# A graph network layer on one core: the node slices move from SyncE's queue to ScalarE's, SyncE copies more rows, and the end of the run is reordered

## The chip, the cores and the metric

One core of a Trainium2 chip. The metric is the time of one execution in device microseconds. Engines are named as in the profile: PE (TensorE), DVE (VectorE), ACT (ScalarE), POOL (GpSimd), SP (SyncE).

## The reference

One message-passing layer with a residual and a normalisation, on 12500 nodes of 64 features and 400000 edges with 16 attributes, sorted by `dst`:

```
m_in     = concatenate([x[src], x[dst], edge_attr], -1)
h        = silu(m_in @ W1 + b1)
messages = silu(h @ W2 + b2)
agg      = segment_sum(messages, dst, num_segments=12500)
y        = silu(concatenate([x, agg], -1) @ W3 + b3)
out      = layernorm(x + y)
```

## The kernel before

**Tiles and octets.** 128 edges are a tile, eight tiles an octet (1024 edges); there are 391 octets, the last of five tiles. Three octets make a chunk. Since `dst` is sorted, an octet's edges end in a window of 48 consecutive nodes. The table `pa = x @ W1[:64]` is made once, in DRAM.

**Four ways to the rows of `pa` for an octet's 1024 sources.** Most tiles are fetched by POOL, one indirect DMA a tile (`gather`, L448). Some pairs of tiles come another way, spread evenly: ACT and DVE put columns of x together in SBUF, one instruction a column (`columns`, L350 reads addresses into registers, L367 and L369 do the work), and SP copies single rows of `pa`, one DMA a row (`rows`, L393 reads 32 addresses, L397 copies). `ROWS` sets how many rows SP copies an octet: 256/15 = 17.07. A pair of tiles that comes one of these ways saves POOL two gathers.

**An octet's way through the engines.** SP loads the slice of x for the octet's window of nodes (`window_load`, L463 to L467; into one of three buffers xr) and, once a chunk, the edge attributes into the lower part of the tile oh (`load`, L485; two buffers, so that a chunk's load follows the last use of the chunk before the previous one). PE multiplies the slice (`window_product`, L472); DVE compares destinations and PE transposes the result (`turn`, L515), DVE copies it into oh (L525). The first layer (`first_layer`) is transposes of the fetched rows (L550), column products (L553) and one large product (L554); ACT makes h of it (L557). The second layer (L566, L568) goes to ACT for m (L572), into a single PSUM buffer p2. PE adds m up by node (`add_up`, L581), DVE adds the window into agg (`add_window`, L592). Finished groups of nodes pass through the last layer and the normalisation and are stored by SP (`store`, L664).

**The order of work.** A loop written by hand (from L757) sets the order on PE, ACT, DVE and SP; POOL's gathers go out ahead. Iteration o issues, among others: the slice for octet o+3, the oh load for the chunk that begins with octet o+3 (when one does, so in every third iteration), gathers for octet o+3, `turn` and `window_product` for o+1, the first layer of o with h, the second layer of o-2 with m, the adding up of o-4, and row copies. On ACT an iteration is: 24 columns, h, 16 columns, m. The oh load of iteration o waits for PE's first layer of octet o-1.

**Eight semaphores.** Every transfer that SP or ACT issues raises one of eight semaphores, named DMAHW0 to DMAHW7 in the listing of the built program. They are given out in turn to the transfers of both engines, in one order that the scheduler makes of the whole program. A transfer waits on its engine until the transfer before it on the same semaphore has landed. Where a row of the listing reads `[waits DMAHW2_49]`, this is that wait.

**The end.** The last iterations use shorter distances (`DRAIN`). `QUIET` keeps the last octets free of columns. At o = 390 the group of nodes `rest` and a check of limits are done, and the window additions of the folding step 391 come in the next turn of the loop; then come the last group, the verdict, the stores, and a load of the verdict on every engine (L106) for the branch into a general version that these inputs don't need.

```
def window_load(o):
    if o % 4 == 0:
        bases(ENG.SP, o)
    xr = xrs[o % 3]
    nc.sync.dma_start(xr[:D, :].bitcast(U8), xt2b[:, ds(winreg.pop((ENG.SP, o)), 8 * S)])
```

Of the kernel before, what the change touches and what calls it, by code (L numbers as in the profile page):

```python
# [12 lines left out]
U8 = mybir.dt.uint8  # L13
# [5 lines left out]
ENG = mybir.EngineType  # L19

P = 128
G = 4
CT = 24
OT = 8
S = 48
# [8 lines left out]
TABLES = 7  # L34
ACOLS = (48, 32)
VCOLS = (32, 0, 32, 32)
ROWS = (256, 15)
LOADS = (16, 32)
XADDR = 16640
X2ADDR = XADDR + 50528  # L40
AADDR = X2ADDR + 50016
HALF = 6144
OVER = 304
TURN = 195
QUIET = 5
DRAIN = 8
LAG = CT * P // 32
AHEADS = 256
# [6 lines left out]
@with_exitstack  # L55
def kernel(
    ctx: ExitStack,
    tc: tile.TileContext,
    x: bass.AP,
    xt: bass.AP,  # L60
    xt2: bass.AP,
    src_c: bass.AP,
    src_row: bass.AP,
    src_pair: bass.AP,
    dst_c: bass.AP,
    dst_row: bass.AP,
    attr_t: bass.AP,
    attr_2: bass.AP,
    base: bass.AP,
    w1: bass.AP,  # L70
    b1: bass.AP,
    w2: bass.AP,
    b2: bass.AP,
    w3: bass.AP,
    b3: bass.AP,
    out: bass.AP,
    edges: int,
):

    nc = tc.nc
    N, D = x.shape

    const = ctx.enter_context(tc.tile_pool(name="const", bufs=1))
    dram = ctx.enter_context(tc.tile_pool(name="dram", bufs=1, space=DRAM))
    pa = dram.tile([N, D], F32, name="pa")
    badi = const.tile([1, 1], I32, name="badi")
    ident = const.tile([P, P], F32, name="ident")
    make_identity(nc, ident)
    identb = const.tile([P, P], BF16, name="identb")  # L100
    nc.vector.tensor_copy(identb, ident)

    with ExitStack() as inner:
        windows(inner, tc, ident, identb, badi, pa, x, xt, xt2, src_c, src_row, src_pair, dst_c, dst_row, attr_t, attr_2, base, w1, b1, w2, b2, w3, b3, out, edges)

    flag = nc.values_load(badi[0:1, 0:1], min_val=0, max_val=4 * P,  # L106
                          skip_runtime_bounds_check_because="a count of partitions")
    with tc.If(flag > 0):
        general(tc, ident, x, xt, src_c, dst_c, dst_row, attr_t, w1, b1, w2, b2, w3, b3, out, edges)


def windows(ctx, tc, ident, identb, badi, pa, x, xt, xt2, src_c, src_row, src_pair, dst_c, dst_row, attr_t, attr_2, base, w1, b1, w2, b2, w3, b3, out, edges):
    nc = tc.nc
    N, D = x.shape
# [3 lines left out]
    NO = base.shape[1]  # L118
# [18 lines left out]
    bi = fast.tile([1, NO], I32, name="bi")  # L137
# [83 lines left out]
    NA = max(HALF + OVER, N - HALF + S)  # L221
# [27 lines left out]
    bi8 = bf.bitcast(I32)  # L249
# [45 lines left out]
    with tc.tile_pool(name="gat", bufs=AHEAD + 2) as gat, \  # L295
# [32 lines left out]
        for eng in counts:  # L328
            pairs[eng] = []
            for o in range(len(octs) - QUIET - 2):  # L330
                if counts[eng][o] >= 2 * P * (len(pairs[eng]) + 1):
# [43 lines left out]
        def rcount(o):  # L375
            return max(0, o - RAW) * ROWS[0] // ROWS[1]

# [57 lines left out]
        winrow, winreg = {}, {}  # L435
        xt2b = xt2.bitcast(U8)
# [16 lines left out]
        def bases(eng, o):  # L453

            n = min(4, NO - o)
            at, least, most = (bi8, 0, 8 * (N - 1)) if eng == ENG.SP else (bi, AADDR, AADDR + 4 * (NA - S))
            _, regs = nc.values_load_multi_w_load_instructions(
                at[0:1, o:o + n], engines=(eng,), min_val=least, max_val=most,
                skip_runtime_bounds_check_because="dst names a node")
            for i in range(n):  # L460
                winreg[eng, o + i] = regs[i]

        def window_load(o):  # L463
            if o % 4 == 0:
                bases(ENG.SP, o)
            xr = xrs[o % 3]
            nc.sync.dma_start(xr[:D, :].bitcast(U8), xt2b[:, ds(winreg.pop((ENG.SP, o)), 8 * S)])  # L467
            winrow[o] = xr

        def window_product(o):  # L470
# [89 lines left out]
        def second_layer(o):  # L560
            c, t0, n, first, last = octs[o]
            n2 = n + n % 2
            k = n2 // 2
            h, eh = made.pop(o)
            p2 = ps2.tile([P, OT, D], F32, name="p2")
            nc.tensor.matmul(p2[:, :n2, :], one3, b2r[:, :n2, :], start=True, stop=False, skip_group_check=True)  # L566
            for i in range(k):
                nc.tensor.matmul(p2[:, 2 * i:2 * i + 2, :].rearrange("p s d -> p (s d)"), h[:, i, :], w2d,  # L568
                                 start=False, stop=(i == k - 1), skip_group_check=True)
            columns(o + 1, ENG.Activation, 1)  # L570
            m = msg.tile([P, OT, D], F32, name="m")
            nc.scalar.activation(m[:, :n2], p2[:, :n2], AF.Silu)  # L572
            made[o] = m, eh

        def add_up(o):
            c, t0, n, first, last = octs[o]
            m, eh = made.pop(o)
            pg = sums[:, o % 4, :]
            for i in range(n):
                s = i % 2  # L580
                nc.tensor.matmul(pg[s * D:(s + 1) * D, :], m[:, i, :], eh[:, i // 2, :, s],  # L581
                                 start=(i < 2), stop=(i >= n - 2), skip_group_check=True)
# [4 lines left out]
        def add_window(o):  # L587
            if o == TURN:
                nc.vector.tensor_copy(agg[:, :OVER], agg[:, HALF:HALF + OVER])
                clear(HALF, NA)  # L590
            a = agg.bitcast(U8)[:, ds((winreg.pop((ENG.DVE, o)) - AADDR).with_bounds(min_val=0, max_val=4 * (NA - S), guaranteed_mod_val=0, out_of_modulus=4), 4 * S)].bitcast(F32)
            nc.vector.tensor_tensor(a, a, sums[:, o % 4, :], op=OP.add)  # L592
# [4 lines left out]
        NG = len(groups)  # L597
        RB = 5
        v = nv.tile([P, 2 * RB, G, D], F32, name="v")
# [56 lines left out]
        def divide(q, i):  # L656
            p = groups[q][1] // G
            vi = v[:p, q % (2 * RB), i, :]
            j = q * G + i
            nc.vector.tensor_scalar(vi, vi, mv[:p, j, 0:1], rstd[:p, j:j + 1], op0=OP.subtract, op1=OP.mult)  # L660

        def store(q):
            c, n = groups[q]
            nc.sync.dma_start(out[c:c + n, :].rearrange("(p i) d -> p i d", i=G), v[:n // G, q % (2 * RB)])  # L664

# [11 lines left out]
        for q in range(rest):  # L679
            o = lead[due[q]] + LAST - 1  # L680
# [10 lines left out]
        for q0, q1 in batches:  # L691
            o = lead[due[q1 - 1]] + LAST + 2 * G
# [27 lines left out]
        def verdict(bad):  # L720
            pc = mis.tile([1, 4], F32, name="mm")
            nc.tensor.matmul(pc, onec, bad, start=True, stop=True)
            bs = nv.tile([1, 1], F32, name="bs")
            nc.vector.tensor_reduce(bs, pc, AX.X, OP.add)
            nc.vector.tensor_copy(badi, bs)

        def times(lags):

            at = {}
            for o in range(NO):  # L730
                at.setdefault(o + lags.get(NO - 1 - o, lags[None]), []).append(o)
            return at
# [3 lines left out]
        folds = times({None: LAST, **{k: 3 for k in range(DRAIN)}})  # L736
# [17 lines left out]
        with tc.manual_schedule(engines={ENG.PE, ENG.Activation, ENG.DVE, ENG.SP}):  # L754
# [4 lines left out]
            for o in range(NO + 2):  # L759
# [3 lines left out]
                for k in range(0, NA, XC)[3 * o - 3:3 * o] if o else []:  # L763
                    n = min(XC, NA - k)
# [33 lines left out]
                for b in range(0, NO, 4):  # L798
                    if o == b + (4 if b < NO - DRAIN else 2):
                        bases(ENG.DVE, b)  # L800
                for q in folds.get(o, []):
                    add_window(q)
                if o == 1:
                    relative(0, CT, SCT)
                for k in range(3 * o - 3, 3 * o) if 1 <= o < 6 else []:
                    if k < 2 * len(parts):
                        c = parts[k // 2]
# [5 lines left out]
                def behind():  # L813
                    for q in adds.get(o, []):
                        add_up(q)
                    for q in seconds.get(o, []):
                        second_layer(q)

                if o == NO - 1:
                    assert NG == rest + 2 and groups[rest][0] + groups[rest][1] + LAG <= (NO - 4) // (CT // OT) * STEP  # L820
                    behind()
                    for i in range(G):
                        node_sums(rest, i)
                    node_silu(rest)
                    node_add(rest)
                    for i in range(G):
                        node_stats(rest, i)
                    bad = limits()
# [42 lines left out]
                if o in (NO - 4, NO - 3):  # L871
                    q = rest + (o == NO - 3)
# [4 lines left out]
            for i in range(NO + 2, NO + LAST):  # L877
                for q in folds.get(i, []):
                    add_window(q)
            assert NO not in todo  # L880
            for i in range(G):
                node_sums(rest + 1, i)
            node_silu(rest + 1)
            node_add(rest + 1)
            for i in range(G):
                node_stats(rest + 1, i)
            verdict(bad)
            root(rest, NG)
            inverse(rest, NG)
            for q in range(rest, NG):  # L890
                for i in range(G):
                    divide(q, i)
                store(q)


@with_exitstack
def general(ctx, tc, ident, x, xt, src_c, dst_c, dst_row, attr_t, w1, b1, w2, b2, w3, b3, out, edges):
# [9 lines left out]
    assert turns * U * P == edges  # L907
    ROWS = N + P

# [3 lines left out]
    pb = dram.tile([N, D], F32, name="gpb")  # L913
    accs = [dram.tile([ROWS, D], F32, name=f"acc{k}") for k in range(NACC)]

# [34 lines left out]
    with tc.tile_pool(name="gpre", bufs=3) as pre, tc.tile_pool(name="zero", bufs=1) as zp, \  # L950
            tc.tile_pool(name="gpre_ps", bufs=4, space=PSUM) as pps:
        width = ROWS * D // P
        assert width * P == ROWS * D
        zero = zp.tile([P, width], F32, name="zero")
# [197 lines left out]
```

## Time and profile before

| | |
|---|---|
| median of 3 runs | 3294.95 us (3292.81 to 3297.97) |
| profiled execution | 3292.35 us, span 3290.6 us |
| mean granted TensorE clock | 0.708 |
| gathers of POOL (L448), both tables | 2599 |
| row copies of SP (L397) | 6400 |
| slices (L467), oh loads (L485) | 391, 132 |
| columns of ACT (L367), of DVE (L369) | 14464, 16000 |

Busy times leave out DMA issues and register loads; these stand in the timeline as SPq and ACTq. A group's row gives its total busy time, the mean of one instruction, the idle time before it and what ended most of that. In the rows of a source line the three numbers are the shortest, the median and the longest duration in ns. A row of a window gives its length and then busy time of PE, PEld, DVE, ACT and POOL, the granted clock, and the DMA share.

### The profile page before, as it was taken

What the parts mean: (1) busy time and instruction counts of PE and PEld (TensorE: products, weight loads), DVE (VectorE), ACT (ScalarE), POOL (GpSimd) and SP (SyncE); (2) the same over time, 40 slices, a digit from 0 to 9 for tenths busy, and PEclk for the clock granted to TensorE, in tenths of its full rate; (3) what the DMA queues carried; (4) which work ended last, traced back from release to release, by engine and by line L of the source; (5) the groups of instructions that cost most, each with busy time, mean ns of one, the idle gap of its engine ahead of it and who ended that gap; (6) DMA issues with size and microseconds to landing.
All of it is one profiled execution on the core that took longest, in us unless ns stands there. A gap on an engine that the chain in (4) does not pass through costs nothing. (4 is left out here: it accounts for less than half of the span.)

```text
span 3290.6 us, 88339 instructions
## 1 busy us (share of the span) xinstructions
PE 2486.1 (76%) x15344; PEld 1705.0 (52%) x15344; DVE 2042.4 (62%) x18296; ACT 3109.2 (94%) x15306; POOL 2465.6 (75%) x2607
## 2 busy tenths in 40 slices
PE   7867777777777777767777777777877867777786
PEld 5545555555555545544454554545545545554554
DVE  5566666666666666666666666666666666666652
ACT  2799999999999999999999999999999999999991
POOL 7777777777777777777777777777777777777774
PEclk8787777777667677677767767766666676667666
DMA  7222222222222222221221222222222222222221
GB/s 148 50 41 40 43 41 40 43 41 40 45 44 44 42 42 40 41 43 38 48 46 39 43 41 40 43 43 43 45 41 42 40 44 41 43 44 45 39 42 33
DMA packets 160868, 147.82 MB, mean 45 GB/s; under 512 B 103748, under 2 KB 113718, under 8 KB 159526
## 3 DMA queue, kind: packets, MB, share of 16 engines
q0 software_dynamic: 83168, 85.33, 14.6%
q1 hardware_dynamic: 62624, 47.00, 5.7%
q10 hardware_dynamic: 14502, 9.75, 1.4%
q14 instruction: 447, 3.66, 0.4%
q8 instruction: 127, 2.08, 0.3%
HBM read 135.44 MB, written 6.40 MB: 43 GB/s over the span
## 5 line engine op out<-in xcount | busy, mean ns | idle before, releaser
L448 POOL DMA_INDIRECT ga<-pa,sc x2505 | 2375.6, 948 | 763.9 <-issue 666.0
L367 ACT ACTIVATE cx<-xs,x 128x1 f32 x14464 | 2789.5, 328 | 24.9 <-issue 19.5
L369 DVE TENSOR_TENSOR cx<-xs,x 128x4 uint8 x16000 | 1288.9, 154 | 1095.6 <-issue 1073.7
L581 PEld LDWEIGHTS pg<-eh,m 128*64 128x64 f32 x6250 | 296.8, 184 | 674.5 <-DVE agg L592 344.5
L550 PE MATMUL p<-ident,ga 128*128 128x128 f32 x1253 | 347.1, 364 | 393.7 <-DMA ga<-pa,sc 392.6
L568 PEld LDWEIGHTS p<-w2d,h 128*128 128x128 f32 x3126 | 536.7, 259 | 186.5 <-issue 186.5
L568 PE MATMUL p<-w2d,h 128*128 128x128 f32 x3126 | 632.5, 365 | 0.0
L554 PE MATMUL p<-oh,xw 128*128 128x512 f32 (+1 forms) x758 | 584.6, 866 | 0.0
L581 PE MATMUL pg<-eh,m 128*64 128x48 f32 x6250 | 352.8, 271 | 211.4 <-DVE agg L592 209.1
L550 PEld LDWEIGHTS p<-ident,ga 128*128 128x128 f32 x1253 | 220.4, 186 | 468.4 <-issue 433.2
L557 ACT ACTIVATE h<-p 128x512 f32<-128x512 f32 x391 | 243.1, 622 | 53.5 <-PE p L554 33.1
L515 PE MATMUL ph<-identb,eh 128*96 128x128 bf16 x1563 | 211.9, 276 | 99.9 <-DVE oh L525 96.4
L572 ACT ACTIVATE m<-p 128x512 f32<-128x512 f32 x391 | 242.6, 620 | 41.6 <-PE p L568 40.0
L525 DVE COPY oh<-ph 96x512 f32<-96x512 f32 x391 | 263.1, 673 | 1.9 <-PE ph L515 1.9
L515 PEld LDWEIGHTS <-eh 128*96 128x96 bf16 x1563 | 163.4, 163 | 136.5 <-DVE oh L525 122.4
L566 PE MATMUL p<-b2r,one 3*128 3x512 bf16 x391 | 193.3, 494 | 53.7 <-ACT m L572 53.2
L472 PE MATMUL mm<-w1bb,xr 65*96 65x128 f32 x782 | 221.5, 377 | 6.6 <-DMA xr<-in_xt 4.0
L497 DVE TENSOR_TENSOR eh<-wrow,dc 128x384 f32<-128x384 f32 x392 | 212.5, 542 | 11.3 <-PE wrow L624 6.9
L554 PEld LDWEIGHTS p<-oh,xw 128*128 128x128 f32 x758 | 175.8, 284 | 0.0
L472 PEld LDWEIGHTS mm<-w1bb,xr 65*96 65x96 f32 x782 | 139.9, 230 | 8.1 <-DMA xr<-in_xt 4.2
L553 PE MATMUL p<-cx,w1d 128*128 128x128 f32 x474 | 122.1, 368 | 0.0
L477 DVE TENSOR_TENSOR xw<-mm,mask 96x128 f32<-96x128 f32 x391 | 108.1, 276 | 20.6 <-PE mm L472 18.0
(106 smaller groups left out, 980.1 us busy)
## 6 DMA issues: line engine op xcount, KB each, us to landing
rx<-pa SPq DMA_DIRECT2D x6400, 0.2 KB
ga<-pa,sc POOLq DMA_INDIRECT x2505
oh<-in_attr SPq DMA_DIRECT2D x130, 192.0 KB
xr<-in_xt SPq DMA_DIRECT2D x391, 24.0 KB
cxi<-in_src_pair SPq DMA_DIRECT2D x238, 1.0 KB
xs<-in_xt ACTq DMA_DIRECT2D x6, 512.0 KB
pa<-v ACTq DMA_DIRECT2D x12, 256.0 KB
x<-in_xt ACTq DMA_DIRECT2D x6, 512.0 KB
```

Of the source, the lines that this page charges most:

```text
L367: nc.scalar.activation(cols[key][:, k:k + 1], word(i, xb, XADDR), AF.Identity, bias=word(i + 4, x2b, X2ADDR))
L369: nc.vector.tensor_tensor(t[:, 4 * k:4 * k + 4], at(i, xb, XADDR), at(i + 4, x2b, X2ADDR), op=OP.max)
L448: nc.gpsimd.indirect_dma_start(out=ga[:, i, :], out_offset=None, in_=x if o < RAW else pa[:, :], in_offset=bass.IndirectOffsetOnAxis(ap=sc ...
L472: nc.tensor.matmul(pw[:E, :], winrow[o], w1bb.rearrange("k s m -> k (s m)"), start=True, stop=True)
L515: nc.tensor.matmul(ph[:E, i, :], eh[:, i, :, 1], identb, start=(i == 0), stop=(i == k - 1), skip_group_check=True)
L525: nc.vector.tensor_copy(oh[:E, :], ph[:E, :(n + 1) // 2].rearrange("p i e -> p (i e)"))
L550: nc.tensor.matmul(p1[:, i, :], g2.rearrange("p s d -> p (s d)"), ident, is_transpose=True, start=(i == c), stop=False, skip_group_check=True)
L554: nc.tensor.matmul(p1[:, :k], xw[o % 3], oh, start=False, stop=True, skip_group_check=True)
L557: nc.scalar.activation(h[:, :k], p1[:, :k], AF.Silu)
L568: nc.tensor.matmul(p2[:, 2 * i:2 * i + 2, :].rearrange("p s d -> p (s d)"), h[:, i, :], w2d, start=False, stop=(i == k - 1), skip_group_ch ...
L572: nc.scalar.activation(m[:, :n2], p2[:, :n2], AF.Silu)
L581: nc.tensor.matmul(pg[s * D:(s + 1) * D, :], m[:, i, :], eh[:, i // 2, :, s], start=(i < 2), stop=(i >= n - 2), skip_group_check=True)
```

## The change

- `window_load` and the register loads of its addresses (`bases`) go to ACT's queue.
- `ROWS` goes from 256/15 to 256/14: 18.29 rows an octet; 26 pairs of tiles instead of 25 come by rows. `QUIET` goes from 5 to 3: one more pair comes by DVE's columns. POOL's gathers from `pa` go from 2505 to 2501.
- At the end: the window additions of step 391 move ahead of the group `rest`, the verdict ahead of the last group's sums, the load of the flag ahead of the last store, and the last store (53 partitions) is split into 48 and 5.

```diff
-ROWS = (256, 15)
+ROWS = (256, 14)
...
-QUIET = 5
+QUIET = 3
...
-            at, least, most = (bi8, 0, 8 * (N - 1)) if eng == ENG.SP else (bi, AADDR, AADDR + 4 * (NA - S))
+            at, least, most = (bi8, 0, 8 * (N - 1)) if eng != ENG.DVE else (bi, AADDR, AADDR + 4 * (NA - S))
...
             if o % 4 == 0:
-                bases(ENG.SP, o)
+                bases(ENG.Activation, o)
             xr = xrs[o % 3]
-            nc.sync.dma_start(xr[:D, :].bitcast(U8), xt2b[:, ds(winreg.pop((ENG.SP, o)), 8 * S)])
+            nc.scalar.dma_start(xr[:D, :].bitcast(U8), xt2b[:, ds(winreg.pop((ENG.Activation, o)), 8 * S)])
...
-            nc.sync.dma_start(out[c:c + n, :].rearrange("(p i) d -> p i d", i=G), v[:n // G, q % (2 * RB)])
+            to, p = out[c:c + n, :].rearrange("(p i) d -> p i d", i=G), n // G
+            for a, b in ((0, p // 16 * 16), (p // 16 * 16, p)):
+                if b > a:
+                    nc.sync.dma_start(to[a:b], v[a:b, q % (2 * RB)])
...
-                for q in folds.get(o, []):
+                for q in folds.get(o, []) if o != NO else []:
                     add_window(q)
...
                     behind()
+                    for q in folds[NO]:
+                        add_window(q)
                     for i in range(G):
                         node_sums(rest, i)
...
+            verdict(bad)
             for i in range(G):
                 node_sums(rest + 1, i)
...
-            verdict(bad)
             root(rest, NG)
...
+                if q == NG - 1:
+                    flag = nc.values_load(badi[0:1, 0:1], min_val=0, max_val=4 * P,
+                                          skip_runtime_bounds_check_because="a count of partitions")
                 store(q)
```

Three places of the listing follow (line numbers of the changed kernel are smaller by two here: L465 is the slice, L395 the row copy, L483 the oh load).

**First place: ACT, around the start of iteration 188.** Before, m of octet 185 is followed at once by the register loads and columns of iteration 188:

```order
L557 ACTIVATE h<-p_94525 128x512 [waits PE_49,Activation_49]
L350 TENSOR_LOAD cxi
L367 ACTIVATE cx<-xs,x_100 128x1 x8
L350 TENSOR_LOAD cxi
L367 ACTIVATE cx<-xs,x_100 128x1 x8
L572 ACTIVATE m<-p_94828 128x512 [waits PE_49,Activation_49]
L350 TENSOR_LOAD cxi
L367 ACTIVATE cx<-xs,x_100 128x1 x8
```

Now:

```order
L555 ACTIVATE h<-p_95131 128x512 [waits PE_49,Activation_49]
L348 TENSOR_LOAD cxi
L365 ACTIVATE cx<-xs,x_100 128x1 x8
L348 TENSOR_LOAD cxi
L365 ACTIVATE cx<-xs,x_100 128x1 x8
L570 ACTIVATE m<-p_95434 128x512 [waits PE_49,Activation_49]
L465 DMA xr_167<-in_xt 64x384 [waits DMAHW7_49,DMAHW2_49]
L348 TENSOR_LOAD cxi
L365 ACTIVATE cx<-xs,x_100 128x1 x8
```

The slice for octet 191 stands between m and the columns, with a wait on DMAHW7 (for the previous transfer into the same buffer) and on DMAHW2, the semaphore that it raises itself.

**Second place: SP, where that slice stood, and where its semaphore is now.** Before, the slice for octet 191 is one of SP's own transfers, between the rows of two iterations:

```order
L397 DMA rx<-pa 1x256 [waits DMAHW6_49]
L397 DMA rx<-pa 1x256 [waits DMAHW7_49]
L467 DMA xr_167<-in_xt 64x384 [waits DMAHW0_49,PE_49]
L397 DMA rx<-pa 1x256 [waits DMAHW1_49]
L397 DMA rx<-pa 1x256 [waits DMAHW2_49]
```

Now, among the row copies of iteration 190 (its first is two rows above these):

```order
L395 DMA rx<-pa 1x256 [waits DMAHW2_49]
L395 DMA rx<-pa 1x256 [waits DMAHW3_49]
L395 DMA rx<-pa 1x256 [waits DMAHW4_49]
L395 DMA rx<-pa 1x256 [waits DMAHW5_49]
L395 DMA rx<-pa 1x256 [waits DMAHW6_49]
L395 DMA rx<-pa 1x256 [waits DMAHW7_49]
L395 DMA rx<-pa 1x256 [waits DMAHW0_49]
L395 DMA rx<-pa 1x256 [waits DMAHW1_49]
L391 TENSOR_LOAD rxi
L395 DMA rx<-pa 1x256 [waits DMAHW3_49]
```

The copies take the semaphores in turn; between the last two DMAHW2 is missing. That is where the scheduler's order has ACT's slice of iteration 188. It therefore waits for the first row shown, the third row copy of iteration 190, and the next copy on DMAHW2 waits for the slice.

**Third place: SP, just ahead of the oh load of iteration 192.** In the changed program:

```order
L395 DMA rx<-pa 1x256 [waits DMAHW0_49]
L395 DMA rx<-pa 1x256 [waits DMAHW1_49]
L395 DMA rx<-pa 1x256 [waits DMAHW2_49]
L395 DMA rx<-pa 1x256 [waits DMAHW3_49]
L395 DMA rx<-pa 1x256 [waits DMAHW4_49]
L395 DMA rx<-pa 1x256 [waits DMAHW5_49]
L395 DMA rx<-pa 1x256 [waits DMAHW6_49]
L424 DMA cxi<-in_src_pair 1x256 [waits DMAHW7_49,DVE_sequencer_49]
L483 DMA oh<-in_attr 32x1536 [waits DMAHW2_49,DVE_49,PE_49]
```

Here DMAHW0 and DMAHW1 are missing ahead of the oh load: they are ACT's slices of iterations 189 and 190, which wait for the first two rows shown. The rows belong to iteration 191. The oh load itself waits for PE's first layer of octet 191.

More of the change, by code (lines that the diff above doesn't have):

```diff
@@ L103 @@
     with ExitStack() as inner:
-        windows(inner, tc, ident, identb, badi, pa, x, xt, xt2, src_c, src_row, src_pair, dst_c, dst_row, attr_t, attr_2, base, w1, b1, w2, b2, w3, b3, out, edges)
-    flag = nc.values_load(badi[0:1, 0:1], min_val=0, max_val=4 * P,
-                          skip_runtime_bounds_check_because="a count of partitions")
+        flag = windows(inner, tc, ident, identb, badi, pa, x, xt, xt2, src_c, src_row, src_pair, dst_c, dst_row, attr_t, attr_2, base, w1, b1, w2, b2, w3, b3, out, edges)
     with tc.If(flag > 0):
@@ L892, in windows @@
                     divide(q, i)
+                if q == NG - 1:
+                    flag = nc.values_load(badi[0:1, 0:1], min_val=0, max_val=4 * P,
+                                          skip_runtime_bounds_check_because="a count of partitions")
                 store(q)
+    return flag
 @with_exitstack
```

## The prediction

> **What bounds the kernel now.** I read first the page's busy shares and its costliest groups, then a stretch of 500 us from the middle, then 18 us of the timeline.
>
> ```profile
> PE 2486.1 (76%) x15344; PEld 1705.0 (52%) x15344; DVE 2042.4 (62%) x18296; ACT 3109.2 (94%) x15306; POOL 2465.6 (75%) x2607
> ...
> L448 POOL DMA_INDIRECT ga<-pa,sc x2505 | 2375.6, 948 | 763.9 <-issue 666.0
> ```
>
> ```profile
> 1500.00:2000.00 500.00, 379.26 (x2346) 254.63 (x2346) 318.68 (x2922) 494.38 (x2448) 378.51 (x399) 0.71 0.21 43
> ```
>
> POOL looks only 75% busy, but behind each gather of 0.95 us stand some 0.3 us of "issue", in which it waits for nothing. In the timeline below two gathers start at 1600.27 and 1601.54, 1.25 us apart, and the stretch holds 399 gathers: 399 x 1.25 = 499 of 500 us. POOL is full. ACT is busy 494.38 of 500 us. With 2599 gathers for 391 octets (6.65 each) the stretch holds 60 octets: **8.33 us an octet for POOL, 8.24 for ACT**. Two engines are full, and the third question is SP, whose queue the shares don't count.
>
> ```profile
> 1599.67 0.48 SPq L467 DMA_DIRECT2D xr<-in_xt  x1
> ...
> 1600.26 5.58 SPq L397 DMA_DIRECT2D rx<-pa  x17
> 1600.27 0.96 POOL L448 DMA_INDIRECT ga<-pa,sc  x1 [0.30 <-issue]
> ...
> 1600.95 0.60 PE L566 MATMUL p<-b2r,one 3*128 3x512 bf16 x1
> ...
> 1601.49 2.08 PE L568 MATMUL p<-w2d,h 128*128 128x128 f32 x8
> 1601.54 0.94 POOL L448 DMA_INDIRECT ga<-pa,sc  x1 [0.30 <-issue]
> ...
> 1603.35 0.63 PE L515 MATMUL ph<-identb,eh 128*96 128x128 bf16 x4
> ...
> 1603.78 0.69 PE L472 MATMUL mm<-w1bb,xr 65*96 65x128 f32 x2
> 1603.83 0.64 ACT L557 ACTIVATE h<-p 128x512 f32<-128x512 f32 x1
> ...
> 1604.26 0.63 PE L550 MATMUL p<-ident,ga 128*128 128x128 f32 x2
> ...
> 1606.01 0.48 SPq L467 DMA_DIRECT2D xr<-in_xt  x1
> ...
> 1606.58 7.77 SPq L397 DMA_DIRECT2D rx<-pa  x17
> ...
> 1607.54 0.65 ACT L572 ACTIVATE m<-p 128x512 f32<-128x512 f32 x1
> ...
> 1608.19 1.91 PE L554 MATMUL p<-oh,xw 128*128 128x512 f32 x2
> ...
> 1614.52 0.47 SPq L467 DMA_DIRECT2D xr<-in_xt  x1
> ```
>
> ```profile
> L350 ACTq TENSOR_LOAD <-cxi x1808: 1002/1020/1264, 89.0 to 3198.0; - x181
> ```
>
> ```profile
> L393 SPq TENSOR_LOAD <-rxi x200: 1868/2126/2337, 140.7 to 3216.0; - x100
> ```
>
> ```profile
> L467 SPq DMA_DIRECT2D xr<-in_xt x391: 468/480/1461, 9.0 to 3230.9; - x196
> ```
>
> ```profile
> L485 SPq DMA_DIRECT2D oh<-in_attr x132: 315/326/1521, 9.6 to 3230.5; - x132
> ```
>
> SP issues 17 row copies in 5.58 us (**0.328 us each**), or in 7.77 us where one TENSOR_LOAD of 2.13 us stands among them; with the slice's 0.48 it has hardly a gap. Counted from the start of the run, the h at 1603.83 is octet 189's, the m at 1607.54 is that of octet 187 and ends ACT's iteration 189, and the slice that SP issues at 1606.01 is that of iteration 190. **So SP begins iteration 190 only 1.5 us before ACT does.** On that lead the whole forecast rests.
>
> **The change part by part.** *The gathers.* Four go (2505 to 2501): one row pair more and one DVE pair more. 4 x 1.25 = 5.0 us less on POOL, its bound. *The end of the run.* Here PE waits for an addition on DVE that is written behind the whole check of limits:
>
> ```profile
> 3269.00 1.10 PE L581 MATMUL pg<-eh,m 128*64 128x48 f32 x16 [4.07 <-DVE agg L592]
> ```
>
> With the addition ahead of the check up to 4.1 us go; what is late next is PE's own chain, so between 0 and 4.1; I take 4. The earlier load of the flag and the split last store come behind one another on SP either way; I take 0 to 2 and put in 0. Together **-9 us**.
>
> *The slice on ACT's queue, alone.* It adds to ACT 391 issues of 0.48 us and 98 small TENSOR_LOADs. ACT's TENSOR_LOADs of 1.02 us run beside the ACTIVATEs (the busy share could not be 99% otherwise, with 4.6 of them an octet), since ACT's queue runs ahead of its arithmetic; the slice's issue should hide in the same way. I cost it at nothing as long as the queue is ahead, and at 391 x 0.48 + 98 x 1.02 = 288 us at most without that cover.
>
> *The wait that comes with it.* The slice's transfer shares the eight semaphores with SP's, and must wait until the previous transfer on its semaphore has landed. Before, that was always an earlier one of SP's own queue. Such waits are real:
>
> ```profile
> SPq L485 <- PE mm L542: 26.2, 3, 11.3
> ...
> SPq L397 <- DMA xr<-in_xt: 5.8, 11, 1.1
> ```
>
> The second row is a row copy held by a slice's landing; the two share no data. In the changed program, counted over the listing, 186 slices stand behind a row copy of SP's **next** iteration and 177 behind one of the **next but one**; 28 behind something older. Iteration 188's slice, at the second place shown above, waits for the third row copy of iteration 190; that of 189, at the third place, for a copy just ahead of the next oh load. In the trace, SP would issue this copy long after ACT needs the slice's place: ACT reaches iteration 190 at 1607.5, and SP gives out the rows of 190 from 1606.58 and those of 191 only after 1614.52. Everything on ACT stands behind that wait: its TENSOR_LOADs, cx columns, h and m, for which PE waits, and with PE the buffers of POOL.
>
> Can SP simply run two iterations ahead? No: every third iteration its load of oh (L485) goes into the buffer that the first layer of the octet before has just read, and waits for PE; the first row of the last fence is such a wait, from the first octets, whose first layer runs through L542. This closes a loop over three octets: first layer of octet 188 on PE, oh load of iteration 189 on SP, the row copies behind it, the slice on ACT, ACT's work, the second layer and then the first layer of octet 191 on PE, which releases the next oh load. Its length, from the rows above:
>
> - SP. For iteration 189's slice a mean of 45 of SP's transfers stand between the oh load and the copy that it waits for (counted over all slices at that place of a loop): 0.33 for oh, 45 x 0.328 = 14.8, 45/32 TENSOR_LOADs of 2.13 = 3.0, and the landing of the last copy. The trace gives no row for that; it lies between 0 and 8 x 0.328 = 2.6, since eight semaphores in turn hardly ever hold a copy; I take the middle, 1.3. Sum **19.4**.
> - ACT. Issue 0.48 and, with the queue run dry, a TENSOR_LOAD of 1.02 and some 0.3 between them, 1.8; one iteration of 8.24; the end of m, 0.65 against the 0.48 at which the next one starts, 0.2. Sum **10.2**.
> - PE. Second layer 0.60 + 2.08, turn 0.63, product 0.69, four transposes 2 x 0.63 at most and 0.85 without their wait, first layer 1.91: **6.8**, and 0.3 for three hand-overs.
>
> 19.4 + 10.2 + 6.8 + 0.3 = **36.7 us for three octets, 12.2 an octet**. The other way round the same loop, by iteration 188's own slice (a mean of 19 transfers: 0.33 + 6.2 + 1.3 + 1.3 = 9.1; ACT two iterations, 1.8 + 16.5 + 0.2 = 18.5; PE 7.1), gives 34.7, 11.6 an octet. The longer one counts. From iteration 12, where rows begin, to about 377, the last octet with a row pair, that is 365 octets x (12.2 - 8.33) = 1412 us more.
>
> The PE rows are from a stretch of low clock. At the end of the run the same eight matmuls took this:
>
> ```profile
> 3258.15 1.16 PE L568 MATMUL p<-w2d,h 128*128 128x128 f32 x8
> ```
>
> 1.16 against 2.08, so at full clock PE's leg is about 3.8 and the loop 33.7 us, 11.2 an octet, 1060 us more; halfway, as the mean granted clock of 0.71 has it, the leg is 5.3 and the loop 35.2, 1240 us more. I take the slow rows, since PE will stand idle for longer stretches than now, and at the end of the run, with PE busy a third of the time, the clock was no higher:
>
> ```profile
> 3260.00:3290.60 30.60, 10.07 (x81) 8.09 (x81) 8.54 (x44) 3.92 (x7) 0.81 (x1) 0.64 0.05 12
> ```
>
> The Trainium skill, "TensorE: Matmul & The Clock Gate", section "Part 1: The HAM clock gate", has the gate fall to half rate after an idle window of about 3.4 us; by it the slow rows stand, by a clock halfway the sum would be 170 us less. The row of 0.64 at low load agrees with it, without proving it.
>
> Sum against the profiled execution (3292.35 us, 2.6 below the median of the runs): 3292 + 1412 - 9 = 4695. **I predict 4700 us.**
>
> **The rivals.** *Faster after all.* If the copies in front of the slices have always landed, nothing waits, and what is left is the gain: 3295 - 9 = 3286 us, 0.3% less. It decides at whether SP can be one to two iterations ahead of ACT when ACT wants to issue. For it speaks that SP is freed of 0.48 us an octet; against it the lead of 1.5 us, the L485 wait, and that one more row copy an octet (0.33 us) eats most of what is freed. Chance 0.08. The Trainium skill, "DMA: Bandwidth & Descriptors", section "Issuing engines are not separate DMA queues", says that issuing from several engines saves only the sequencer's time; that rule alone leads to this rival, and no run yet shows which holds.
>
> *The issue's own price.* No loop, but ACT's queue is not ahead at the slice and its arithmetic stops for the whole issue: 3295 + 288 - 9, about 3570. Against it: an ACT that reads 16 addresses in 1.02 us beside its arithmetic. Chance 0.03.
>
> *A looser loop.* The loop closes only for some thirds (the slices behind the next iteration alone, not the next but one), and ACT catches up between: about half of the 1412, 4000 us. Chance 0.05. *A longer one*, where the 50 and more transfers that half of the slices have in front of them set the pace: 5 x 0.4 us more each loop, and late addresses on top: over 5000. Chance 0.03.
>
> **How the numbers follow.** Forecast 0.81: 4300 (full clock: 3292 + 1060 - 9 = 4343) to 5000 (5 more transfers and 2.6 instead of 1.3 for the landing: 36.7 + 3.3 = 40.0 us, 13.3 an octet, 1825 more, if all loops had it; half of them have). About 0.8 lies in it, so that it is the range too. A measurement tells 0.2% of this kernel from no change: faster 0.06 and same 0.02 (both from the first rival), slower 0.92.
>
> **What would show it.** Right: SP's own waits led by the oh load on PE, ACT idle before its cx columns without anything that its arithmetic waits for, POOL waiting for PE's release of ga, ACT's share down to about 66% and POOL's to 53%, and about 36 us for three octets, even from start to end. Wrong: ACT at 94% as now, gathers still 1.25 us apart, and SP's row copies running on at 0.328 us; then the time is about 3286. If the time is in the range but the slices wait for something else than row copies, the sum was right by chance.

## The result, and the profile after

The changed kernel takes **4747.57 us** (median of 5 runs, 4741.67 to 4755.89) where the kernel before takes 3294.95 (5 runs, 3292.81 to 3297.97): a ratio of **1.4411, with a 95% interval of 1.4393 to 1.4429**. The profiled execution has a span of 4739.9 us and a mean granted clock of 0.673.

From the page of the changed kernel, the busy shares and two groups:

```profile
PE 2467.4 (52%) x15345; PEld 1791.0 (38%) x15345; DVE 2072.2 (44%) x18426; ACT 3124.4 (66%) x15306; POOL 2456.4 (52%) x2603
...
L446 POOL DMA_INDIRECT ga<-pa,sc x2501 | 2366.5, 946 | 2221.0 <-PE p L548 1466.6
```

Every engine is busy for as many microseconds as before (ACT 3124 against 3109, POOL 2456 against 2466), so no piece of work became dearer. The shares fell because the span grew. POOL's gather still takes 0.946 us; its idle time, which used to be led by 0.3 us of "issue" a gather, is now led by PE.

A stretch of 500 us from the middle shows the same by rate (length, then PE, PEld, DVE, ACT, POOL, clock, DMA share, GB/s):

```profile
1500.00:2000.00 500.00, 242.91 (x1524) 177.11 (x1524) 209.74 (x1914) 324.59 (x1607) 246.31 (x261) 0.66 0.11 27
```

261 gathers against 399: 39 octets in 500 us where there were 60. Who waits for whom, from the waits of the changed kernel (us in total, times, longest):

```profile
PE p L564 <- ACT m L570: 2151.3, 337, 17.2
POOL ga L446 <- PE p L548: 1466.6, 215, 17.4
ACT cx L365 <- issue: 874.6, 140, 12.5
ACT cx L365 <- DMA rx<-pa: 472.4, 62, 12.7
```

Read from the top: POOL waits for PE, PE for ACT's m, and ACT stands ahead of its columns. The columns need no data from row copies (rx); the profile names a row copy because its landing is the last event before ACT goes on. "issue" is the same place where it could name nobody: the instruction that waits is the slice's DMA in front of the columns, which isn't counted as ACT's work. Now SP's own waits:

```profile
SPq L483 <- PE p L552: 1129.7, 125, 16.2
SPq L483 <- DVE oh L523: 481.5, 85, 26.1
```

The oh load (L483) holds SP for 1611 us in all. Before, its largest row was 26.2 us. That is the circle, and the timeline shows one turn of it:

```profile
2317.13 0.32 SPq L483 DMA_DIRECT2D oh<-in_attr  x1
...
2317.54 14.38 SPq L395 DMA_DIRECT2D rx<-pa  x37
...
2325.32 0.50 ACTq L465 DMA_DIRECT2D xr<-in_xt  x1
...
2332.68 5.81 SPq L395 DMA_DIRECT2D rx<-pa  x18
...
2337.42 0.48 ACTq L465 DMA_DIRECT2D xr<-in_xt  x1
...
2339.04 4.55 ACT L365 ACTIVATE cx<-xs,x 128x1 f32 x24 [3.59 <-issue]
...
2347.21 0.58 ACT L570 ACTIVATE m<-p 128x512 f32<-128x512 f32 x1
...
2347.84 0.58 PE L564 MATMUL p<-b2r,one 3*128 3x512 bf16 x1 [6.61 <-ACT m L570]
...
2348.35 2.08 PE L566 MATMUL p<-w2d,h 128*128 128x128 f32 x8
...
2352.19 1.54 PE L552 MATMUL p<-oh,xw 128*128 128x512 f32 x2
...
2353.76 0.33 SPq L483 DMA_DIRECT2D oh<-in_attr  x1
```

SP issues an oh load at 2317.13 and then row copies. The slice at 2337.42 goes out only when the copy in front of it on its semaphore has landed, 20.3 us after the oh load. The single records name the semaphore that a transfer raises: the copy in front of this slice was issued from 2336.24 to 2336.47, a row of SP's next iteration but one; the copy in front of the slice at 2325.32 was issued from 2324.11 to 2324.34. ACT then needs until 2347.79 for its iteration (10.4 us), PE until 2353.73 for second and first layer (5.9 us), and 0.03 us later SP may issue the next oh load. **36.6 us for three octets.** Over 90 such turns, octets 60 to 330, the mean between two oh loads is 36.9 us (24.7 before), and the three slices of a turn go out 9.3, 20.7 and 28.5 us behind the oh load (worked out from all records of L483 and L465). Behind the issue of the copy in front of it on its semaphore the first slice goes out 1.2 us and the second 1.0 us (medians over the same turns), so these two wait for row copies; the third goes out 8.4 us behind and finds its copy landed.

### The profile page after: what moved, and what is told of

The parts are those of the page before. It is cut to its first block, busy times and chain, and to the rows that moved or that the text cites. A ratio compares the mean times of both kernels' runs of the same rounds, so it can differ in the third digit from the quotient of the medians.

```text
span 4739.9 us, 88994 instructions
## 1 busy us (share of the span) xinstructions
PE 2467.4 (52%) x15345; PEld 1791.0 (38%) x15345; DVE 2072.2 (44%) x18426; ACT 3124.4 (66%) x15306; POOL 2456.4 (52%) x2603
## 3 DMA queue, kind: packets, MB, share of 16 engines
q8 instruction: 127, 2.08, 0.2%
## 5 line engine op out<-in xcount | busy, mean ns | idle before, releaser
L365 ACT ACTIVATE cx<-xs,x 128x1 f32 x14464 | 2760.2, 284 | 1490.7 <-issue 874.6
L566 PEld LDWEIGHTS p<-w2d,h 128*128 128x128 f32 x3126 | 599.7, 286 | 2311.5 <-issue 2311.1
L566 PE MATMUL p<-w2d,h 128*128 128x128 f32 x3126 | 704.0, 395 | 0.0
L552 PE MATMUL p<-oh,xw 128*128 128x512 f32 (+1 forms) x758 | 556.5, 828 | 0.0
L579 PEld LDWEIGHTS pg<-eh,m 128*64 128x64 f32 x6250 | 243.0, 154 | 476.3 <-issue 275.7
L579 PE MATMUL pg<-eh,m 128*64 128x48 f32 x6250 | 293.2, 240 | 48.5 <-DVE agg L590 47.8
L548 PE MATMUL p<-ident,ga 128*128 128x128 f32 x1251 | 307.2, 382 | 0.0
L523 DVE COPY oh<-ph 96x512 f32<-96x512 f32 x391 | 263.4, 674 | 1.6 <-PE ph L513 1.6
L548 PEld LDWEIGHTS p<-ident,ga 128*128 128x128 f32 x1251 | 244.5, 209 | 0.0
L590 DVE TENSOR_TENSOR agg<-agg,pg 128x48 f32 x391 | 75.4, 193 | 310.8 <-PE wrow L628 288.2
L513 PEld LDWEIGHTS <-eh 128*96 128x96 bf16 x1563 | 190.5, 180 | 43.5 <-DVE oh L523 27.3
```

The source lines that it names most:

```text
L365: nc.scalar.activation(cols[key][:, k:k + 1], word(i, xb, XADDR), AF.Identity, bias=word(i + 4, x2b, X2ADDR))
L513: nc.tensor.matmul(ph[:E, i, :], eh[:, i, :, 1], identb, start=(i == 0), stop=(i == k - 1), skip_group_check=True)
L523: nc.vector.tensor_copy(oh[:E, :], ph[:E, :(n + 1) // 2].rearrange("p i e -> p (i e)"))
L548: nc.tensor.matmul(p1[:, i, :], g2.rearrange("p s d -> p (s d)"), ident, is_transpose=True, start=(i == c), stop=False, skip_group_check=True)
L552: nc.tensor.matmul(p1[:, :k], xw[o % 3], oh, start=False, stop=True, skip_group_check=True)
```

## The experiments

*The chips.* The runs came to several chips. The chip of e5 to e8 runs the kernel before in 3296.31 us (median of 11 runs), like the chip of the first result. On three others the kernel before itself takes 4883 us (e1 to e4), 4965 us (e9 to e11) and 4949 us (e12). Times expected in microseconds are for a chip with 3295; on those three only ratios and differences to the kernel before on the same chip are read. What slows them is looked at in the last section.

**The same instructions, the semaphores handed out octet by octet.** One line in the loop, and nothing else:

```diff
                 if o == RAW:
                     nc.vector.memset(mv, 1.0)
                     nc.vector.memset(eps, 1e-5)
+                tc.no_sync_barrier()
                 index(o + 3)
```

It adds no transfer and no arithmetic: the traces of the two programs differ by 40 of some 89,000 instructions, all of them semaphore instructions. It keeps the scheduler from ordering one iteration's transfers among the next one's when it hands out the eight semaphores: 366 of 391 slices now stand behind row copies of the iteration before (364 by the records of e5). ACT, SP and POOL have the instructions of the changed kernel in the same order; on PE and DVE two neighbours change places.

> The changed kernel with a fence for the scheduler alone at the start of each iteration: the same instructions in the same order on ACT, SP and POOL (two neighbours on PE and DVE change places), no wait added, but the semaphores are now given out iteration by iteration, so that 366 of the 391 slices stand behind a row copy of the iteration before, which SP issued long ago. Theory one: the loop is gone and the gain is left: 3286 us, 3280 to 3330. Theories two and three, and any price of the transfer on ACT's queue as such: unchanged at 4750 us, or 3570 where only the issue counts.

> The fenced kernel once more, beside runs of the kernel before: the changed kernel's instructions in the same order on every engine, but a line between two octets across which the shared DMA semaphores are handed out octet by octet, so that a slice stands behind row copies of the octet before it and not behind later ones. Where the kernel before takes about 3295 us: the theory that the slowdown comes only from slices standing behind later row copies gives 3280 to 3330 (ratio 0.996 to 1.01), gathers 1.25 us apart again, SP's waits no longer led by the oh load. The theory that the issue on ScalarE has a price of its own gives 3500 to 3600 (ratio about 1.08). The theory that a DMA of two queues contends in itself, whatever the semaphores, gives the changed kernel's 4750 (1.44).

Measured: e3 4882.7 against 4882.8 us, ratio 1.0008 (0.9993 to 1.0023); e5 **3286.55 against 3296.31 us, ratio 0.9969 (0.9957 to 0.998)**. In e5 the page, the stretch of 500 us and SP's waits are those of a kernel that doesn't stand still:

```profile
PE 2486.3 (76%) x15345; PEld 1755.1 (53%) x15345; DVE 2053.5 (63%) x18426; ACT 3102.1 (94%) x15306; POOL 2465.6 (75%) x2603
```

```profile
1500.00:2000.00 500.00, 373.88 (x2354) 265.82 (x2355) 321.75 (x2948) 493.99 (x2455) 378.56 (x399) 0.71 0.21 43
```

```profile
SPq L395 <- DMA xr<-in_xt: 109.6, 104, 3.1
SPq L483 <- DVE oh L523: 82.8, 7, 19.0
...
SPq L483 <- PE p L552: 26.5, 8, 7.4
```

399 gathers again, and the oh load's waits of 1611 us are down to about 110. The waits on shared semaphores haven't gone: the first row is a row copy of SP behind a slice of ACT, the other direction, 104 times and never more than 3.1 us; in the time they cost nothing that is seen. ACT and SP of e5:

```profile
1604.41 0.48 ACTq L465 DMA_DIRECT2D xr<-in_xt  x1
...
1604.99 0.61 ACT L570 ACTIVATE m<-p 128x512 f32<-128x512 f32 x1
...
1605.28 0.32 SPq L483 DMA_DIRECT2D oh<-in_attr  x1
...
1606.27 4.55 ACT L365 ACTIVATE cx<-xs,x 128x1 f32 x24 [0.67 <-issue]
```

The slice now goes out ahead of the m behind which it is written, as ACT's queue runs ahead of its arithmetic, and ahead of the next oh load. So the order in which semaphores are handed out is the whole slowdown: 1.44 with one order, 0.997 with the other, with the same work (each against the kernel before on its own chip). A price of the issue itself (1.08) and contention of two queues as such (1.44) both fall. This version is also faster than both kernels, than the kernel before by 0.3%.

**Everything but the move.** ROWS, QUIET and the end as changed; the slice stays on SP:

```diff
...
-                bases(ENG.Activation, o)
+                bases(ENG.SP, o)
...
-            nc.scalar.dma_start(xr[:D, :].bitcast(U8), xt2b[:, ds(winreg.pop((ENG.Activation, o)), 8 * S)])
+            nc.sync.dma_start(xr[:D, :].bitcast(U8), xt2b[:, ds(winreg.pop((ENG.SP, o)), 8 * S)])
```

> The whole change except the move: the slice stays on SP, which copies 18.3 rows an octet, with the new end. Theory one: no transfer of ACT is left in the loop, so what remains is the gain of four gathers and of the end, 9 us: 3286 us (3280 to 3292). Theory two: the same. Theory three (SP overloaded): SP has 18.29 x 0.328 + 0.57 x 2.13 + 0.48 + some 0.6 for the rest = 8.3 us an octet, as much as the octet takes; if that is too much, 0.1 to 0.4 us an octet late: 3330 to 3450 us.

> Everything of the change but the move: 18.3 rows an octet on SP, four gathers fewer, the end ordered anew, the slice still issued by SP. By my sum 4 x 1.25 + 4 = 9 us less than before, so about 3286 (ratio 0.997) on a chip where the kernel before takes 3295. The rival is that SP, with 1.2 row copies an octet more (0.4 us of 8.33), becomes the bound: then 365 octets x up to 0.4 us, up to 3440 (ratio up to 1.045). If the end alone does nothing, 3290.

Measured: e2 5014.44 us, ratio 1.0264 (1.025 to 1.0277); e6 **3418.62 us, ratio 1.0375 (1.0361 to 1.039)**. My forecast for this run, 3286, was wrong and its rival right. The stretch, a wait and SP's queue of e6:

```profile
1500.00:2000.00 500.00, 340.18 (x2223) 236.18 (x2222) 308.98 (x2810) 472.64 (x2340) 359.21 (x379) 0.73 0.20 41
```

```profile
PE mm L470 <- DMA xr<-in_xt: 579.0, 238, 6.9
```

```profile
1601.67 0.33 SPq L483 DMA_DIRECT2D oh<-in_attr  x1
1602.10 0.48 SPq L465 DMA_DIRECT2D xr<-in_xt  x1
1605.05 6.12 SPq L395 DMA_DIRECT2D rx<-pa  x18
1612.10 0.51 SPq L465 DMA_DIRECT2D xr<-in_xt  x1
```

SP issues without a break but for its TENSOR_LOADs (one of 2.1 us fills most of the 2.5 ahead of 1605.05), and PE waits for slices that SP sends too late. 1.22 rows an octet more are 1.22 x (0.328 + 2.13/32) = 0.48 us on an SP that had nothing left. The window gives 500/379 x 6.64 = 8.76 us an octet against 8.33, 0.43 more (2595 gathers for 391 octets are 6.64 each). So the move pays for the rows: 0.48 us of slice for 0.48 us of rows. Without the move the rest costs 122 us; with it, and the semaphores in order, all together gains 9.8.

**The move alone.** The kernel before with `bases` and the slice on ACT, ROWS, QUIET and the end as before (the lines of the diff above, the other way).

> The kernel before with the slice and its addresses on ACT's queue and nothing else. Theory one (a loop through the shared semaphores: oh load, row copies, slice, ACT's work, first layer): 176 slices stand behind a row copy of SP's next iteration and 199 behind one of the next but one, as in the whole change, with 17.07 instead of 18.29 rows an octet on SP's leg; its 19.4 us become about 18.3, the loop 35.6 us, 11.9 an octet: 4500 to 4750 us. Theory two (the slice's issue and address loads cost ACT their own time): at most 3295 + 288 = 3580 us. Theory three (the 18.3 rows overload SP, or the new end costs): 3295 us, no change.

> The kernel before with nothing changed but the slice and its addresses on ScalarE's queue; 17.07 rows an octet. The loop theory: SP's leg has about 42 transfers instead of 45, 18.3 us instead of 19.4, the loop 35.8 instead of the 36.9 that the changed kernel showed, 11.9 an octet: 3292 + 365 x (11.9 - 8.33) = 4600, within 4500 to 4720. The rival by which row count or the new end carry a good part of the slowdown: under 4400. A fixed price of the issue: about 3580.

> The kernel before with the move of the slice alone, once more. Where the kernel before takes about 3295 us: the loop theory gives 4500 to 4720 (loop 35.8 us for three octets, 42 transfers in SP's leg instead of 45), with slices standing about 8.5 and 19.5 us behind the oh load. If the row count or the new end carry a good part of the slowdown, under 4400; a fixed price of the issue gives about 3580. Where the kernel before takes 4900 or more: 5700 to 5900, as the two runs so far.

Measured: 5744.95, 5870.77 and 5854.74 us where the kernel before takes 4882.78, 4965.18 and 4949.21: 862, 906 and 906 us more, ratios 1.18. All three fell on the slow chips, so the 4500 to 4720 us were not tried. What they do show is that the move alone brings the circle: in e12 the oh load again leads SP's waits,

```profile
SPq L485 <- PE p L554: 941.7, 89, 19.7
```

and its slices go out 14.5, 26.9 and 35.4 us behind it in a turn of 44.8 us (means over the same octets as above).

**Half the rows.** The changed kernel with

```diff
-ROWS = (256, 14)
+ROWS = (256, 28)
```

> The changed kernel with a row pair in every second place only (one pair of 28 edges' share where there were two), so that SP copies about half as many rows and GpSimd gathers the rest. In the loop of three octets SP's leg falls from 19.4 us to about 0.33 + 22 x 0.328 + 1.5 + 1.3 = 10.4 us, the loop from 36.7 to about 28 us or, by the other way round (ACT's two iterations and half of 6.2 us), about 31 us: 10.3 an octet, 3292 + 365 x 2.0 and the added gathers: 3900 to 4350. The theory of a fixed price for each wait on the other queue, whatever stands in front, gives the changed kernel's 4750 or a little under it.

Measured: 4127.87 us (one run), inside 3900 to 4350. One turn of e7:

```profile
2016.79 0.32 SPq L483 DMA_DIRECT2D oh<-in_attr  x1
...
2025.12 0.49 ACTq L465 DMA_DIRECT2D xr<-in_xt  x1
...
2033.24 0.48 ACTq L465 DMA_DIRECT2D xr<-in_xt  x1
...
2043.27 0.59 ACT L570 ACTIVATE m<-p 128x512 f32<-128x512 f32 x1
...
2050.21 0.33 SPq L483 DMA_DIRECT2D oh<-in_attr  x1
```

The second slice comes 8.1 us behind the first, which is ACT's own pace, and over 90 turns the first goes out 1.2 us and the second 7.5 us (medians) behind the issue of the copy in front of it. So here only the first one waits, and the turn goes the other way round: 8.3 us of SP, 18.7 of two iterations on ACT, 6.3 of PE. Its mean over 90 turns is 31.7 us, where the expectation had 31. The price follows what stands in front of the slice and is no fixed one for a wait. Of its parts SP's 8.0 us (mean) is more than half of 9.3: though SP copies half as many rows, 15.8 of its transfers stand between the oh load and the end of the copy in front of the first slice, against 19.5 in the changed kernel.

**The oh load octet by octet.** Six small buffers instead of two large ones, the same bytes:

```diff
-            tc.tile_pool(name="hot", bufs=2) as hot, \
+            tc.tile_pool(name="hot", bufs=6) as hot, \
...
-                if o + 3 < NO and octs[o + 3][3]:
-                    load(octs[o + 3][0])
+                if o + 3 < NO:
+                    load(o + 3)
...
```

> The changed kernel with the oh tile loaded octet by octet into six small buffers instead of three octets at a time into two: the same bytes, 391 loads instead of 132, and a load waits only for the first layer of six octets before it. If the oh load's wait for PE closes the loop, the loop now spans six octets with one oh wait each: less than the changed kernel, 4000 to 4500. If the wait on the oh buffer is only a symptom (SP held by something else), the time stays at 4750. If the loop is gone altogether (SP free to run ahead), about 3400.

Measured: 4330.38 us (one run), inside 4000 to 4500. SP's waits of e8:

```profile
SPq L424 <- ACTq L348: 339.7, 51, 14.4
SPq L391 <- DVE eh L492: 262.5, 19, 23.1
SPq L661 <- DVE agg L586: 259.2, 19, 21.6
SPq L424 <- DVEq L348: 123.9, 21, 16.5
SPq L480 <- PE p L548: 118.2, 60, 7.7
```

The oh load (L480 here) is no longer what holds SP most. In its place stand a load of addresses (L424) that waits until ACT has read the old ones, SP's own reading of row addresses (L391), and stores (L661), both of them named with DVE. So the oh load is the tightest link but not the only one. That the circle closes through the next links is read from these rows and not shown: no run loosened them too.

**No row copies.** The changed kernel with `ROWS = (256, 100000)`: POOL gathers every row, 52 gathers more than the changed kernel (2553 against 2501 from `pa`; the second expectation has 46).

> The changed kernel without row copies (SP copies none; 26 pairs of tiles go back to POOL, 2647 gathers from both tables instead of 2595). Theory one: no row copies stand in front of the slices; the loop has only index and oh loads in SP's leg and is far shorter than 25 us; POOL sets the time: 3292 + 48 x 1.25 - 4 for the end = 3348 us (3335 to 3370). Theory two: 288 us more, 3640. If the slice's transfers on ACT's queue collide with anything else than row copies, still over 4000.

> The changed kernel without row copies: GpSimd gathers every edge row (some 46 gathers more than the changed kernel, 58 us at 1.25 us each), the slice still on ScalarE. SP's leg of the loop is empty, so the theory gives the kernel before plus 58 less 4: 3340 to 3380 (ratio 1.015 to 1.025). If two queues' DMAs cost something in themselves, or the issue on ScalarE has its price of up to 288 us, 3600 and more.

Measured: e4 4133.37 us, ratio 0.8462 (0.8449 to 0.8475); e11 4171.66 against 4965.18 (one run). Both fell on the slow chips and are there 15 to 16% *faster* than the kernel before, so on those chips row copies are a good part of what is slow, though not all: 4133 us is still far above the 3348 expected where the kernel before takes 3295. With the slice on ACT and no rows in front of it no circle is left to see: ACT's longest wait ahead of its columns is 1.9 us in e4, against 12.7 in the changed kernel. The 3340 to 3380 us expected of the other chips were not tried, nor were no rows with the slice on SP, so these runs don't price the move.

**The end, without rows and move.** Before, with the end reordered (the diff's last six pieces). `QUIET` is 3 here, as in the changed kernel, so that POOL also has two gathers fewer than before (2503 from `pa`): the end is not quite alone, other than the expectation says.

> Only the end of the run ordered anew; rows (17.07 an octet) and the slice stay as in the kernel before. My sum gave the end 0 to 4.1 us, taken as 4: ratio 0.9988, with the interval of a measurement (0.1%) just short of or just over 'no change'. If the whole 9.8 us by which the fenced kernel is faster comes from the end, the ratio is 0.997; if the end gives nothing and the four gathers (5 us) and a freer SP give the rest, 1.000.

Measured: 4958.54 against 4965.18 us, ratio 0.9991 (0.9982 to 1.0): 6.6 us less, with an interval that reaches to nothing, and two gathers of 1.25 us may be in it. The traces show the end better. The last h and the last z, first of the kernel before, then of the changed one (with the product of an earlier first layer ahead of them, which the step on the clock uses):

```profile
3264.96 0.49 ACT L557 ACTIVATE h<-p 128x384 f32<-128x384 f32 x1 [0.60 <-PE p L554]
...
3275.05 0.38 ACT L636 ACTIVATE z<-mm 53x256 f32<-53x256 f32 x1 [2.36 <-PE mm L630]
```

```profile
4712.49 1.02 PE L552 MATMUL p<-oh,xw 128*128 128x512 f32 x2
...
4721.18 0.49 ACT L555 ACTIVATE h<-p 128x384 f32<-128x384 f32 x1 [0.60 <-PE p L552]
...
4727.28 0.38 ACT L634 ACTIVATE z<-mm 53x256 f32<-53x256 f32 x1 [3.82 <-PE mm L628]
```

10.1 us became 6.1 (5.05 in e5). The stretch behind it shrank too: from the last z to the end of the span (3290.6 and 4739.9 us) 15.5 us became 12.6 (12.2 in e5). The ten profiles with the new end lie between 11.1 and 12.6 there, the four with the old one between 15.1 and 15.8. What the change touches there is the verdict, the load of the flag and the last store; no run separates them.

## Why the prediction was right, step by step

- *The bound.* POOL, ACT and SP were full, and SP the third: shown by e6, where 0.48 us more on SP lengthens an octet of the middle by 0.43.
- *Gathers and end, -9 us.* e5 is 9.8 us faster than before, with an interval of 6.6 to 14.2, so the sum is right, but by luck: its parts are not. From the last h to the end of the span the profile of before has 25.6 us and that of e5 17.3, 8.3 less where the prediction had 4. Of these 5.0 are the wait for the addition, put at 4 of at most 4.1, and 3.3 lie behind the last z, the step with the flag and the stores that was put at 0. The gathers' 5.0 are not seen: POOL's last gather ends 2.3 us earlier in e5, but the last h begins 2.6 us later (one profile each, of kernels whose runs spread by 3 to 9 us).
- *The issue on ACT, nothing.* In e5 ACT is busy 493.99 of 500 us with all slices on its queue, against 494.38 before. Right. But the prediction nowhere priced the added rows *without* the move: it said that they eat most of what is freed. e6 shows that they eat all of it.
- *The wait through shared semaphores.* Shown by e5: only the handing-out of semaphores differs, and 1461 us go (4747.57 to 3286.55, each on a chip of its own; the kernel before differs by 1.4 between them). The records of the changed kernel also have the slices where the prediction put them: 184 stand behind a row copy of SP's next iteration and 175 behind one of the next but one (186 and 177 by the listing), and two of each turn's three go out about 1 us behind that copy's issue.
- *The circle of three octets.* Forecast 36.7 us, mean measured 36.9. Its terms: SP 19.4 forecast, 20.7 measured (mean); ACT 10.2 against 10.4 in the turn shown; PE with hand-overs 7.1 against 5.9. In SP's term the landing, put at 1.3, is not what was short: the second slice goes out 1.0 us behind the issue of the copy in front of it (median; mean 1.45). The issuing is: up to the end of that copy's issue SP takes 19.2 us with 46.8 transfers (means), where the sum had 18.1 with 45. An SP term that is 1.3 short and a PE term that is 1.2 long cancel, so that the sum is better than its parts, which is luck. The slice of the other way round was put at 9.1 us behind the oh load and stands at 9.3.
- *The clock.* I took PE's slow rows. In the turn above the second layer takes 2.08 us, as slow as forecast, but the first layer 1.54, between the 1.91 of the slow rows and the 1.02 that the same pair takes at 4712.49 in the changed kernel, so PE's leg of 5.9 lies between the slow sum of 7.1 and that of a clock halfway (5.3, with the hand-overs 5.6). The Trainium skill, "TensorE: Matmul & The Clock Gate", section "Part 1: The HAM clock gate", has the gate fall after an idle window of about 3.4 us and rise after about as long a busy one. The turn agrees with it: PE idle for 6.61 us, then eight matmuls at 2.08, and faster ones 4.4 us after work began. The granted clock was 1.00 from 2341.2 to 2346.0, 0.61 from there to 2347.84, 0.50 until 2352.19 and 0.66 while the first layer ran.
- *The signs.* ACT at 66% and POOL at 52% came as said (66% and 53%), as did SP's waits led by the oh load on PE, and POOL's for PE. Not named was DVE's copy into oh (L523), which ends 85 of the oh load's waits, 481 of 1611 us.
- *Only the oh load closes the circle:* too simple. e8 loosens it and 1034 us of the slowdown stay.
- *The rivals.* "Faster after all" at 3286 was rightly put as the case in which the copies in front have always landed: e5 makes that case, and takes 3286.55. The Trainium skill, "DMA: Bandwidth & Descriptors", section "Issuing engines are not separate DMA queues", says that issuing from several engines saves only the sequencer's time. e5 against e6 agrees, 132 us saved where 391 issues of 0.48 us are 188; the changed kernel shows what this rule leaves out, since there the two sequencers stop one another.

## What to carry to other kernels

Before a transfer moves to another engine's queue, look up in the listing which transfer stands in front of it on its completion semaphore, on which engine, and whether that one is issued earlier *in time*; a wait on a transfer that the other queue issues an iteration later makes the two queues one, and any wait of the slower one becomes a wait of both. If a kernel becomes much slower while every engine's busy microseconds stay the same, search for such a circle: take the queue that waits most, follow one turn in the timeline, and see whether its legs add up to the period. Sometimes the cure is only an order in which the semaphores are handed out, and costs nothing.

## What the runs showed of the hardware that was not expected

Three of the chips that the runs came to run the kernel before 48 to 51% slower. There, in the trace of e9, SP's row copies come in fits, and at times all engines stop together. From its timeline, with slices and rows as before:

```profile
2003.33 17.26 SPq L395 DMA_DIRECT2D rx<-pa  x17
...
2008.60 0.94 POOL L446 DMA_INDIRECT ga<-pa,sc  x1 [0.30 <-issue]
2011.43 0.21 DVE L590 TENSOR_TENSOR agg<-agg,pg 128x48 f32 x1 [8.81 <-remote]
2011.45 0.60 ACT L570 ACTIVATE m<-p 128x512 f32<-128x512 f32 x1 [5.12 <-remote]
```

17 row copies take 17.26 us where they took 5.58; DVE and ACT stand until 2011.4, and what ended it is no engine or queue that the profile knows. Between 1000 and 2500 us SP of e9 has 597 gaps of over 0.25 us, mostly of 0.70; the kernel before has 65 on the first chip, of 0.35, and 48 of these just 128 instructions of SP apart (from all records of SP). A single gather takes 0.94 us on either. The cause stays open. For the reader it means that a ratio is read on the chip that gave it: the fenced kernel is 0.3% faster than before on one and no faster on another, and the kernel without row copies, by my sum 2% slower than before on a chip like the first, is 15% faster there.
